# Transformers in a one-core kernel: weight and table loads get an issue-order edge behind a slot's moves, and the second transformer's feed-forward runs one slot earlier

## The chip, the cores and the metric

The kernel runs on one core of a Trainium2 chip. The metric is the device time of the whole program in microseconds (us), taken as the median of several runs. Before the change the median is 4267.34 us (three runs: 4264.73, 4267.34 and 4271.99). A profiled execution of the same program took 4258.36 us; its span, from the first instruction to the last, is 4256.7 us. All times inside the program below are counted from the start of that span.

The engines are named as the profile names them: PE multiplies matrices (PEld loads the weights for it), DVE, ACT and POOL work elementwise, and SP issues DMAs. DMAs can also be issued from the ACT and POOL queues.

## The reference

The input is a stream `x` of 4 rows of 512 tokens with 128 features, in float32. Four layers follow each other, each of the form `x = x + s * silu(f)`, where `s` comes from an attention-like block and `f` from a feed-forward-like block, both of the normalised `x`. The change touches two of these blocks, which are small transformers of their own. They differ in depth, number of heads and window:

| | "l2" (third layer) | "l3" (fourth layer) |
|---|---|---|
| depth | 6 | 2 |
| heads of 64 | 16 | 8 |
| attention window | 32 tokens | 64 tokens |

One layer of such a transformer, cut to what matters:

```
h = shift(x)                      # half of the features come from the token before
q, k, v = split(h @ Wqkv)
q = rotate(l2norm(q) * q_scale)   # cos/sin tables, xpos scaling
k = rotate(l2norm(k) * k_scale)
p = softmax(8 * q @ k.T)          # over the own window and the one before
x = x + (p @ v) @ Wo
h = layernorm(shift(x)) * g + b   # feed-forward
a, gate = split(h @ W1 + b1)
x = x + (a * gelu(gate)) @ W2 + b2
```

## The kernel before

The class `_Transformer` runs each of the two transformers in *slots*. A slot is one triple of layer `l`, row `b` (of 4) and group `gp` of 8 heads. "l2" has two groups (`GP` = 2) and so 6 x 4 x 2 = 48 slots; "l3" has one group (`GP` = 1) and 2 x 4 = 8 slots. Three Python generators make the work, and `transformer` (L707) merges them slot by slot:

- `queries_keys` (L1263) projects a slot's queries and keys (matmuls `S<-hb,l_wqk`), squares them on ACT (`sqp`), multiplies by two rotary tables on DVE (`l_rot<-S,l_tab` L1289, `rotp<-S,l_tab` L1291), adds on POOL (L1292), and normalises (`unit_length`, L1302, with DVE at L1316). Then eight DMAs, the *moves* (`l_qk<-l_rot`, L1323), put the heads where the attention needs them. There are eight for the queries and eight for the keys of a slot, so 896 in all; they are issued from SP.
- `attention` (L1463) works one slot behind. For each slot it first projects the values (`values`, L1326, matmuls `S<-l_wv,hb`), copies them out on ACT, and shifts them with DMAs `l_ve<-l_vo` (L1346 to L1350). Then come the scores (L1377), the softmax, the transposes (`S<-core,l_P`), the weighing with the values (`S<-l_ve,l_PT` and `S<-l_vo,l_PT`), the transposes back (`core,l_On`), and the output projection (`M<-l_OT,l_wo`). Each of these steps lags one or two units behind the scores, so a slot's attention ends early in the slot after.
- `feed_forward` (L1506) works on a row after its attention. Its matmuls are `S<-hb,l_k` and `S<-ffg,core` (layer norm), `S<-hb,l_w` (W1) and `M<-ffu,l_w` (W2).

In slot number i the loop of `transformer` gives `merge` the projection of slot i, the attention of slot i-1 and, from slot `GP + 2` on, the feed-forward. For "l3" the feed-forward of row r is therefore in slot r+3, and the loop has 11 slots. `merge` interleaves the generators by the weights they yield.

The written order is not the order on the engines. The framework that builds the program places each engine's instructions ahead of time, by its own model of when each is ready; the order in which they are written is a priority only. An instruction that waits for nothing, such as a load into a free buffer, so moves forward in its queue. What was placed once stands: on the chip each engine and each queue works strictly in that order, and waits on semaphores at its head.

Weights are loaded on first use by `part` (L1217): `l_wqk` (512 KB, two buffers), `l_wv` (256 KB, two buffers) and `l_wo` (256 KB, two buffers), all from SP. The feed-forward's `W1` and `W2` come from `ff_weights` (L1247), with one buffer each. The rotary tables (1024 KB each, one for queries and one for keys per layer, three buffers) are loaded by `tables` (L1235) from the ACT queue, and are multiplied by the layer's scale on DVE right after (L1243). PSUM has three two-bank tiles `S` and two one-bank tiles `M` for all of these matmuls.

Before "l2" starts, two 1 MB arrays (`away_x`, `away_s`) are written out from SP, and the transformer's column constants `l_cols` take memory that is free once `away_s` is written.

Of the kernel before, what the change touches and what calls it, by code (L numbers as in the profile page):

```python
# [38 lines left out]
class Net:  # L39
# [667 lines left out]
    def transformer(self, pre, depth, heads, window, consts):  # L707

        with ExitStack() as stack:
            pool = lambda name, bufs=1, **kw: stack.enter_context(self.pool(pre + name, bufs, **kw))
            pools = [pool("ps", 3, space=PSUM), pool("pm", 2, space=PSUM), pool("c"), pool("tab", 3), pool("w")]
            pools += [pool("qk", 4), pool("v", 2), pool("p", 2), pool("t", 2)]
            t = _Transformer(self, pre, heads, window, pools, consts)
            t.exp_tables()
            rows = [(l, b) for l in range(depth) for b in range(B)]
            passes = t.queries_keys(rows), t.attention(rows), t.feed_forward(rows)  # L720
            slots = len(rows) * t.GP
            for i in range(slots + t.GP + 2):
                run = []
                if i < slots:
                    run.append((until_none(passes[0]), 10.3))
                if 0 < i <= slots + 1:
                    run.append((until_none(passes[1]), t.attention_weight))
                if i >= t.GP + 2:
                    run.append((until_none(passes[2]), t.feed_forward_weights[i % t.GP]))
                merge(run)  # L730

# [435 lines left out]


class _Transformer:
    def __init__(self, net, pre, heads, window, pools, consts):  # L1170
        self.net, self.nc, self.a, self.pre = net, net.nc, net.a, pre
        self.heads, self.W, self.inner = heads, window, heads * 64
        self.GP = heads // 8
        self.NB = 128 // window
        self.split = self.NB == 4
        self.PS, self.PM, C, self.TB, self.WT, self.QK, self.VP, self.PP, self.TP = pools
        nc, a = self.nc, self.a
        self.T = 4 if self.split else 2
        self.NU = self.T * 64 // window
        self.cols = net.load(C, a[pre + "cols"], name=pre + "_cols")  # L1180
        k = net.load(C, a[consts][:, 0:256], name=pre + "_k", queue=nc.scalar)
        self.ones, self.cen = k[:, 0:128], k[:, 128:256]
        self.tiny = C.tile([128, 1], F32, name=pre + "_tiny")
        nc.vector.memset(self.tiny, 1e-36)
        n = NT // self.T
        self.mask = C.tile([128, n, 512], BF16, name=pre + "_mask")
        nc.gpsimd.dma_start(self.mask, a[consts][:, 256 : 256 + 512 * n].rearrange("p (t n) -> p t n", t=n))
        self.identb = C.tile([128, 128], BF16, name=pre + "_identb")
        nc.vector.tensor_copy(self.identb, net.ident)

        self.ve = [C.tile([128, self.NU, 1024 // self.NB], F32, name=f"{pre}_ve{i}") for i in range(2)]
        for i in range(2 if self.split else 1):
            for lo, hi in self.second():
                nc.gpsimd.memset(self.ve[i][lo:hi, 0, :], 0.0)
        self.made, self.weights = {}, {}

        self.attention_weight = 25.0
        self.feed_forward_weights = (1.7, 7.7) if self.GP == 2 else (9.4,)
        self.y = net.xn

    def second(self):
# [15 lines left out]
    def part(self, kind, l, gp):  # L1217
# [14 lines left out]
            self.weights[key] = t  # L1232
        return self.weights[key]

    def tables(self, l, i):  # L1235

        if ("tab", l, i) not in self.weights:
            nc, pre = self.nc, self.pre
            tab = self.TB.tile([128, 2, 2, S], F32, name=pre + "_tab")
            nc.scalar.dma_start(tab, self.a["k_rot_" + pre][:, 4 * i : 4 * i + 4, :].rearrange("p (m h) s -> p m h s", m=2))  # L1240
            for h in range(2):
                v = tab[:, :, h, :]
                nc.vector.tensor_scalar(v, v, self.col(l, 9 + 2 * i + h), None, ALU.mult)  # L1243
            self.weights["tab", l, i] = tab
        return self.weights["tab", l, i]

    def ff_weights(self, l):  # L1247
        if ("ff", l) not in self.weights:
# [14 lines left out]
    def queries_keys(self, rows):  # L1263


        net, nc, W = self.net, self.nc, self.W
        for l, b in rows:
            hb = net.shifted(net.tok(self.y, b), self.TP, 3)

            hk = hb.rearrange("p (u s k) -> p s u k", s=2, k=W)  # L1270
            for gp in range(self.GP):
                w = self.part("qk", l, gp)
                before = None
                made = []
                for i in range(2):
                    tab = self.tables(l, i)
                    t = self.TP.tile([128, 2, 2, S], F32, name=self.pre + "_rot", bufs=2)
                    sums = []
                    for g in range(2):
                        p = self.S2()  # L1280
                        for h in range(2):
                            c = 128 * (4 * g + 2 * i + h)
                            o = p[:, h, :]
                            net.mm(o.rearrange("p (s u k) -> p s u k", s=2, k=W) if i else o, w[:, c : c + 128], hk if i else hb)
                            yield 0.86
                        sq = self.TP.tile([128, 2, S], F32, name="sqp", bufs=3)
                        nc.scalar.activation(sq, p, AF.Square)  # L1287
                        nc.gpsimd.tensor_tensor(sq[:, 0, :], sq[:, 0, :], sq[:, 1, :], ALU.add)  # L1288
                        nc.vector.tensor_tensor(t[:, g], p, tab[:, 0], ALU.mult)  # L1289
                        m = self.TP.tile([128, 2, S], F32, name="rotp", bufs=1)  # L1290
                        nc.vector.tensor_tensor(m, p, tab[:, 1], ALU.mult)  # L1291
                        nc.gpsimd.tensor_tensor(t[:, g], t[:, g], m[:, ::-1, :], ALU.add)  # L1292
                        sums.append(sq)
                        if before:
                            made.append((yield from self.unit_length(*before)))
                            before = None
                    before = sums, t
                made.append((yield from self.unit_length(*before)))
                self.made[l, b, gp] = hb, made
                yield None  # L1300

    def unit_length(self, sums, t):  # L1302

        net, nc = self.net, self.nc
        p = self.S2()
        for g in range(2):
            net.mm(p[:, g, :], self.ones, sums[g][:, 0, :])
            yield 0.86  # L1310
        rn = self.TP.tile([128, 2, S], F32, name="rn", bufs=1)
        nc.scalar.activation(rn, p, AF.Ln, bias=self.tiny)  # L1312
        nc.scalar.activation(rn, rn, AF.Exp, scale=-0.5)  # L1313
        for g in range(2):

            nc.vector.scalar_tensor_tensor(  # L1316
                t[:, g], rn[:, g, :].unsqueeze(1).to_broadcast([128, 2, S]), 1e12, t[:, g], ALU.min, ALU.mult
            )
        out = self.QK.tile([128, 2, 2, S], F32, name=self.pre + "_qk")
        for r in range(4):  # L1320
            for h in range(2):
                x = 32 * (2 * (r % 2) + h)
                nc.sync.dma_start(out[x : x + 32, :, r // 2, :], t[32 * r : 32 * r + 32, :, h, :])  # L1323
        return out

    def values(self, w, hb, tp, ve):  # L1326
# [136 lines left out]
    def attention(self, rows):  # L1463
# [6 lines left out]
        for i in range(len(units) + 2):  # L1470
# [18 lines left out]
            if older:  # L1489
                if older["j"] == 0:  # L1490
                    OT = self.TP.tile([128, 4, 128 * T], F32, name=self.pre + "_OT", bufs=1)
                self.turn_back(older, OT)
                yield 0.9 if self.split else 0.45
                if older["j"] == 1:
                    wo = self.part("o", older["l"], older["gp"])
                    p = self.M()[:, 0 : 128 * T]
                    for t in range(4):
                        net.mm(p, wo[:, t, :], OT[:, t, :], t == 0, t == 3)
                        yield 0.86 if self.split else 0.43
                    ys = net.tok(self.y, older["b"])[:, 128 * T * older["tp"] : 128 * T * (older["tp"] + 1)]  # L1500
                    nc.vector.tensor_tensor(ys, ys, p, ALU.add)
                older.clear()
            if last:
                yield from self.weigh(last)

    def feed_forward(self, rows):  # L1506
        net, nc = self.net, self.nc
        for l, b in rows:
            w1, w2 = self.ff_weights(l)
            yb = net.tok(self.y, b)  # L1510
            hb = net.shifted(yb, self.TP, 3)
# [178 lines left out]
```

## Time and profile before

| | us |
|---|---|
| median of three runs | 4267.34 |
| profiled execution | 4258.36 |
| its span | 4256.7 |
| PE busy | 3632.9 (85%) |
| DVE busy | 2521.8 (59%) |
| ACT busy | 1832.3 (43%) |
| POOL busy | 1200.4 (28%) |
| "l2" runs from about | 1590 to 3690 |
| "l3" runs from about | 3774 to 4244 |

The key moves of a slot give a clock for the slots. The first one of "l2" starts at 1635.4 and the last at 3633.2: 47 slots in 1997.8 us, 42.5 us each. In "l3" the distances from one slot's key moves to the next are 45.5, 51.6, 53.0, 54.7, 54.9, 54.6 and 51.2 us, from 3811.6 to 4177.1; what is left after that takes until 4244.

In a row of the windows view the columns are the stretch, its length, the busy time of PE, PEld, DVE, ACT and POOL with the number of instructions, the granted share of the PE clock, the share of time the DMA engines were busy, and GB/s. In a timeline a row has its start, its length, the engine, the line, the operation, what it writes and reads, how often, and in brackets the idle time before it with what ended that.

### The profile page before, as it was taken

What the parts mean: (1) busy time and instruction counts of PE and PEld (TensorE: products, weight loads), DVE (VectorE), ACT (ScalarE), POOL (GpSimd) and SP (SyncE); (2) the same over time, 40 slices, a digit from 0 to 9 for tenths busy, and PEclk for the clock granted to TensorE, in tenths of its full rate; (3) what the DMA queues carried; (4) which work ended last, traced back from release to release, by engine and by line L of the source; (5) the groups of instructions that cost most, each with busy time, mean ns of one, the idle gap of its engine ahead of it and who ended that gap; (6) DMA issues with size and microseconds to landing.
All of it is one profiled execution on the core that took longest, in us unless ns stands there. A gap on an engine that the chain in (4) does not pass through costs nothing.

```text
span 4256.7 us, 105246 instructions
## 1 busy us (share of the span) xinstructions
PE 3632.9 (85%) x46765; PEld 1894.8 (45%) x46891; DVE 2521.8 (59%) x3429; ACT 1832.3 (43%) x2495; POOL 1200.4 (28%) x994
## 2 busy tenths in 40 slices
PE   7887999898999986888888888888888888768888
PEld 4554555344444433444444444444444444334444
DVE  6665555205433516677677777777667676447775
ACT  3344666331333343444444444444444444424554
POOL 1011444100111224333333433343333333033221
PEclk7678999996989988999999999999999999879999
DMA  1000000000000004334233424333333332222221
GB/s 35 7 24 26 1 1 1 28 10 7 1 3 2 1 15 113 85 81 106 70 89 98 95 67 120 70 86 94 86 73 92 87 85 69 75 85 68 58 63 43
DMA packets 123574, 236.11 MB, mean 55 GB/s; under 512 B 29625, under 2 KB 44129, under 8 KB 117729
## 3 DMA queue, kind: packets, MB, share of 16 engines
q1 hardware_dynamic: 114064, 209.58, 20.3%
q10 hardware_dynamic: 8624, 19.29, 1.4%
q8 instruction: 369, 6.05, 0.6%
q0 software_dynamic: 432, 0.51, 0.1%
q14 instruction: 85, 0.69, 0.1%
HBM read 50.08 MB, written 5.54 MB: 13 GB/s over the span
## 4 chain that ended last, share of the span: by engine, by line
PE 53%; DVE 16%; ACT 16%; issue 8%; POOL 3%; DMA 3%; SPq 1%; DVEq 0%; POOLq 0%; ACTq 0%
PE S L122 29%; PE M L122 8%; PE S L126 4%; PE S L1377 3%; PE o L1092 3%; DVE l_rot L1316 3%; DVE rotp L1291 3%; ACT l_P L581 3%; DVE l_rot L1289 2%; ACT l_PT L1412 2%; PE o L614 2%; ACT rn L1312 2%; POOL l_rot L1292 2%; ACT sqp L1287 1%; ACT l_P L1396 1%
## 5 line engine op out<-in xcount | busy, mean ns | idle before, releaser
L1292 POOL TENSOR_TENSOR l_rot<-l_rot,rotp 128x1024 f32<-128x1024 f32 x224 | 533.3, 2381 | 459.1 <-DVE rotp L1291 421.6
L1288 POOL TENSOR_TENSOR sqp<-sqp 128x512 f32<-128x512 f32 x224 | 315.6, 1410 | 1010.2 <-ACT sqp L1287 1009.6
L122 PE MATMUL S<-hb,l_wqk 128*128 128x512 f32 x896 | 501.4, 659 | 108.4 <-ACT l_vo L1344 32.3
L1287 ACT ACTIVATE sqp<-S 128x1024 f32<-128x1024 f32 x224 | 229.3, 1024 | 411.0 <-PE S L122 408.6
L1316 DVE SCALAR_TENSOR_TENSOR l_rot<-rn,l_rot 128x1024 f32<-128x1024 f32 x224 | 366.2, 1672 | 64.8 <-ACT rn L1313 62.3
L1289 DVE TENSOR_TENSOR l_rot<-S,l_tab 128x1024 f32<-128x1024 f32 x224 | 272.9, 1218 | 163.7 <-ACT sqp L1287 161.8
L126 PE MATMUL S<-core,l_P 128*128 128x128 f32 x1856 | 269.5, 288 | 57.3 <-DVE rotp L1291 13.5
L122 PE MATMUL S<-l_KT,l_QT 32*128 32x256 f32 (+7 forms) x1536 | 261.9, 505 | 34.8 <-ACT l_P L1114 14.2
L126 PEld LDWEIGHTS S<-core,l_P 128*128 128x128 f32 x1856 | 211.3, 146 | 177.2 <-issue 67.4
L1291 DVE TENSOR_TENSOR rotp<-S,l_tab 128x1024 f32<-128x1024 f32 x224 | 271.6, 1213 | 22.0 <-POOL l_rot L1292 21.8
L122 PE MATMUL S<-sqp,l_k 128*128 128x512 f32 x448 | 241.7, 633 | 33.3 <-POOL sqp L1288 24.9
L1114 ACT ACTIVATE l_P<-S 128x1024 f32<-128x1024 f32 x160 | 156.7, 1022 | 254.6 <-PE S L122 254.5
L1377 PE MATMUL S<-l_qk 64*32 64x64 f32 (+1 forms) x13312 | 222.1, 236 | 43.3 <-issue 34.3
L122 PEld LDWEIGHTS S<-hb,l_wqk 128*128 128x128 f32 x896 | 150.1, 199 | 244.0 <-issue 102.2
L122 PE MATMUL S<-l_wv,hb 128*64 128x256 f32 (+1 forms) x1600 | 237.1, 403 | 7.8 <-ACT rn L1312 2.4
L1377 PEld LDWEIGHTS S<-l_qk 64*32 64x32 f32 (+1 forms) x13312 | 174.1, 110 | 154.5 <-issue 151.0
L1412 ACT COPY l_PT<-S 128x1024 f32<-128x1024 f32 x128 | 129.5, 1012 | 250.1 <-PE S L126 250.0
L1067 DVE TENSOR_REDUCE l_mx<-S 128x2 f32<-128x768 f32 (+1 forms) x192 | 154.9, 863 | 134.1 <-PE S L1006 134.1
L1398 DVE TENSOR_REDUCE rs<-l_P 128x16 f32<-128x1024 f32 (+1 forms) x128 | 155.8, 1217 | 124.2 <-ACT l_P L1396 124.1
L122 PE MATMUL M<-l_OT,l_wo 128*128 128x512 f32 (+1 forms) x512 | 222.7, 546 | 4.1 <-ACT l_OT L1461 2.2
L1118 POOL TENSOR_SCALAR_AFFINE_SELECT l_P<-l_P 128x256 f32<-128x256 f32 x256 | 99.4, 406 | 409.9 <-ACT l_P L1114 405.1
L1387 DVE TENSOR_REDUCE mx<-S 128x16 f32<-128x1024 f32 (+1 forms) x128 | 155.7, 1217 | 98.7 <-PE S L1377 98.5
(359 smaller groups left out, 6619.9 us busy)
## 6 DMA issues: line engine op xcount, KB each, us to landing
l_qk<-l_rot SPq DMA_DIRECT2D x896, 128.0 KB
l_ve<-l_vo SPq DMA_DIRECT2D x112, 256.0 KB
l_ve<-l_vo SPq DMA_DIRECT2D x96, 224.0 KB
l_tab<-in_k_rot_l ACTq DMA_DIRECT2D x16, 1024.0 KB
l_wqk<-in_l2Wqkv SPq DMA_DIRECT2D x12, 512.0 KB
l_wv<-in_l2Wqkv SPq DMA_DIRECT2D x12, 256.0 KB
l_wo<-in_l2Wo SPq DMA_DIRECT2D x12, 256.0 KB
l_ve<-l_vo SPq DMA_DIRECT2D x24, 128.0 KB
```

The lines of the kernel that those rows point to most:

```text
L122: self.nc.tensor.matmul(out, lhsT, rhs, start=start, stop=stop)
L126: self.nc.tensor.transpose(out, in_, self.ident[:n, :n])
L1114: nc.scalar.activation(P[u], s[u], AF.Exp, scale=scale)
L1287: nc.scalar.activation(sq, p, AF.Square)
L1288: nc.gpsimd.tensor_tensor(sq[:, 0, :], sq[:, 0, :], sq[:, 1, :], ALU.add)
L1289: nc.vector.tensor_tensor(t[:, g], p, tab[:, 0], ALU.mult)
L1291: nc.vector.tensor_tensor(m, p, tab[:, 1], ALU.mult)
L1292: nc.gpsimd.tensor_tensor(t[:, g], t[:, g], m[:, ::-1, :], ALU.add)
L1316: nc.vector.scalar_tensor_tensor(t[:, g], rn[:, g, :].unsqueeze(1).to_broadcast([128, 2, S]), 1e12, t[:, g], ALU.min, ALU.mult)
L1377: net.nc.tensor.matmul(sv[W * bl : W * bl + W, e, t, g, :].rearrange("p (s k) -> p s k", s=2), qk[0][r, g, j, W * c : W * c + W], kw, star ...
L1398: nc.vector.tensor_reduce(rs, P.rearrange("p t g e k -> p (t g e) k"), axis=AX.X, op=ALU.add)
L1412: self.nc.scalar.copy(u["PT"], t)
```

## The change

Five edits:

1. Tables are loaded by a new function `load_tables`, from SP instead of ACT. The scaling on DVE stays in `tables`, at first use.
2. A new function `ahead` is called at the end of each slot's projection, inside `issue_after`: every DMA that it traces on SP is placed behind the slot's last move. No completion is waited for; it is an edge of issue order alone. After the slot of row 3 it loads the next layer's `l_wqk` of this group and the table of this group's number (for "l3", both tables). After the slots of row 0 it loads this layer's `l_wv` of this group. `l_wo` follows after (row 0, group 1) and (row 1, group 0), for "l3" after row 0.
3. `ahead` also asks for the feed-forward's weights after row 2. `feed_forward` has asked for the same weights in an earlier place of the merged order (slot 8l+4 against 8l+5 in "l2"; in "l3" at 60% of the same slot), so this adds nothing.
4. In "l3" the feed-forward begins in slot 2 instead of slot 3, with a first `yield 14.0` out of a weight of 23.4 (before: 9.4), so that a row's feed-forward follows in the last 40% of the slot in which its attention ends. The loop has 10 slots instead of 11. In "l2" the slots stay as they were.
5. An `assert` states that the row's attention has been written before; it makes no instruction.

The first layer's `l_wqk` and tables are still loaded without the edge, on first use.

```diff
-            for i in range(slots + t.GP + 2):
+            for i in range(slots + 4 if t.GP == 2 else slots + 2):
...
-                if i >= t.GP + 2:
+                if i >= (4 if t.GP == 2 else 2):
...
-        self.feed_forward_weights = (1.7, 7.7) if self.GP == 2 else (9.4,)
+        self.feed_forward_weights = (1.7, 7.7) if self.GP == 2 else (23.4,)
...
+    def load_tables(self, l, i):
+        if ("tab", l, i) not in self.weights:
+            tab = self.TB.tile([128, 2, 2, S], F32, name=self.pre + "_tab")
+            self.nc.sync.dma_start(
+                tab, self.a["k_rot_" + self.pre][:, 4 * i : 4 * i + 4, :].rearrange("p (m h) s -> p m h s", m=2)
+            )
+            self.weights["tab", l, i] = tab, []
+        return self.weights["tab", l, i]
+
     def tables(self, l, i):
 
-        if ("tab", l, i) not in self.weights:
-            nc, pre = self.nc, self.pre
-            tab = self.TB.tile([128, 2, 2, S], F32, name=pre + "_tab")
-            nc.scalar.dma_start(tab, self.a["k_rot_" + pre][:, 4 * i : 4 * i + 4, :].rearrange("p (m h) s -> p m h s", m=2))
+        tab, ready = self.load_tables(l, i)
+        if not ready:
             for h in range(2):
                 v = tab[:, :, h, :]
-                nc.vector.tensor_scalar(v, v, self.col(l, 9 + 2 * i + h), None, ALU.mult)
-            self.weights["tab", l, i] = tab
-        return self.weights["tab", l, i]
+                self.nc.vector.tensor_scalar(v, v, self.col(l, 9 + 2 * i + h), None, ALU.mult)
+            ready.append(True)
+        return tab
+
+    def ahead(self, l, b, gp):
+
+        last = gp == self.GP - 1
+        if b == B - 1 and l + 1 < self.depth:
+            self.part("qk", l + 1, gp)
+            for i in (gp,) if self.GP == 2 else (0, 1):
+                self.load_tables(l + 1, i)
+        if b == 0:
+            self.part("v", l, gp)
+        if self.GP == 1 and b == 0:
+            self.part("o", l, 0)
+        if self.GP == 2 and (b, gp) in ((0, 1), (1, 0)):
+            self.part("o", l, b)
+        if b == 2 and last:
+            self.ff_weights(l)
...
                 self.made[l, b, gp] = hb, made
+                with net.tc.issue_after(self.move.ins):
+                    self.ahead(l, b, gp)
                 yield None
...
-                nc.sync.dma_start(out[x : x + 32, :, r // 2, :], t[32 * r : 32 * r + 32, :, h, :])
+                self.move = nc.sync.dma_start(out[x : x + 32, :, r // 2, :], t[32 * r : 32 * r + 32, :, h, :])
...
         for l, b in rows:
+            if self.GP == 1:
+
+                yield 14.0
+            assert (l, b) in self.attended
             w1, w2 = self.ff_weights(l)
```

More of the change, by code (lines that the diff above doesn't have):

```diff
@@ L716, in transformer @@
             pools += [pool("qk", 4), pool("v", 2), pool("p", 2), pool("t", 2)]
-            t = _Transformer(self, pre, heads, window, pools, consts)
+            t = _Transformer(self, pre, depth, heads, window, pools, consts)
             t.exp_tables()
@@ L1169, with __init__ @@
 class _Transformer:
-    def __init__(self, net, pre, heads, window, pools, consts):
+    def __init__(self, net, pre, depth, heads, window, pools, consts):
         self.net, self.nc, self.a, self.pre = net, net.nc, net.a, pre
-        self.heads, self.W, self.inner = heads, window, heads * 64
+        self.depth, self.heads, self.W, self.inner = depth, heads, window, heads * 64
         self.GP = heads // 8
@@ L1194, in __init__ @@
                 nc.gpsimd.memset(self.ve[i][lo:hi, 0, :], 0.0)
-        self.made, self.weights = {}, {}
+        self.made, self.weights, self.attended = {}, {}, set()
         self.attention_weight = 25.0
-        self.feed_forward_weights = (1.7, 7.7) if self.GP == 2 else (9.4,)
+        self.feed_forward_weights = (1.7, 7.7) if self.GP == 2 else (23.4,)
         self.y = net.xn
@@ L1501, in attention @@
                     nc.vector.tensor_tensor(ys, ys, p, ALU.add)
+                    if (older["gp"], older["tp"]) == (self.GP - 1, n - 1):
+                        self.attended.add((older["l"], older["b"]))
                 older.clear()
```

## The prediction

> **What bounds the kernel now.** I read the page first (busy shares and the chain that ended last), then the windows by stage, then the waits, then timelines of the queues and engines that the change touches.
>
> ```profile
> PE 3632.9 (85%) x46765; PEld 1894.8 (45%) x46891; DVE 2521.8 (59%) x3429; ACT 1832.3 (43%) x2495; POOL 1200.4 (28%) x994
> ...
> PE 53%; DVE 16%; ACT 16%; issue 8%; POOL 3%; DMA 3%; SPq 1%; DVEq 0%; POOLq 0%; ACTq 0%
> ```
>
> PE is the busiest engine and holds half of the chain; DMA and SP's queue hold 4% together. That is the first warning: a change that orders loads has little waiting to remove.
>
> ```profile
> 1635.00:3633.00 1998.00, 1711.03 (x29006) 875.71 (x29095) 1406.26 (x1505) 902.92 (x1019) 721.05 (x420) 0.98 0.36 86
> ...
> 3812.00:3857.00 45.00, 35.12 (x314) 20.30 (x316) 32.42 (x39) 20.17 (x25) 15.44 (x9) 0.92 0.29 68
> 3857.00:3909.00 52.00, 40.49 (x352) 24.42 (x356) 35.66 (x42) 21.95 (x29) 15.80 (x9) 0.87 0.25 59
> 3909.00:4177.00 268.00, 234.09 (x1880) 133.60 (x1901) 199.38 (x240) 144.03 (x175) 73.85 (x49) 0.96 0.27 63
> 4177.00:4219.00 42.00, 39.33 (x409) 25.49 (x410) 25.09 (x37) 22.66 (x34) 0.09 (x1) 1.00 0.21 48
> 4219.00:4244.00 25.00, 20.91 (x41) 8.15 (x40) 8.44 (x15) 10.50 (x13) 0.00 (x0) 0.86 0.00 0
> ```
>
> The first number after the length is PE's busy time: 86% through "l2", 87% in the full slots of "l3", 78% in its filling (3812 to 3909), 94% and 84% in its draining. So both transformers are near PE's pace, with about 6 us idle in a slot of 42.
>
> ```profile
> SPq L1323 <- DVE l_rot L1316: 817.4, 86, 26.2
> ...
> SPq L1224 <- PE S L122: 87.8, 5, 19.4
> ```
>
> SP waits for `l_wqk`'s buffer at the head of its queue (87.8 us, 5 times), but the moves behind are not held: by the timeline each batch leaves within 0.4 us of the DVE result (L1316) it carries, and summed over all 112 batches the lateness is 3 us. What the edge would protect is not being lost.
>
> **A. The values' weights come late.** This is the large term. `l_wv` was loaded a layer ahead; now it may leave only behind the key moves of the slot whose values come next.
>
> ```profile
> 1958.76 0.38 SPq L1231 DMA_DIRECT2D l_wo<-in_l2Wo  x1
> 1959.94 12.58 SPq L1323 DMA_DIRECT2D l_qk<-l_rot  x16
> 1975.69 1.20 SPq L1346 DMA_DIRECT2D l_ve<-l_vo  x2
> ```
>
> ```profile
> 1964.12 0.65 PE L122 MATMUL S<-l_wv,hb 128*64 128x256 f32 x4
> 1964.71 1.98 PE L122 MATMUL S<-hb,l_w 128*128 128x512 f32 x4
> 1966.62 1.51 PE L122 MATMUL S<-l_wv,hb 128*64 128x256 f32 x12
> ...
> 1972.56 1.95 PE L122 MATMUL S<-l_wv,hb 128*64 128x256 f32 x16
> ```
>
> The last move leaves SP at 1972.5, `l_wv` at 1973.0 (0.53 us is the median of its issue rows). A 1024 KB table took 4.9 us from its issue (1892.76) to the DVE row that it released (1897.65); 256 KB lie between a quarter of that and all of it, and I take 3 us, so 1976. The values' matmuls ran from 1964.12 to 1974.50: they would start 12 us late, 4.1 us of PE work (0.65 + 1.51 + 1.95). The planner sees this and puts other ready work there: W1 (5.6 us), the next slot's queries (2 us a tile), transposes (1.1 each way), weighing (2.5). These cover nearly all 12 us, but PSUM has only three `S` tiles, and PE's order is then fixed, so a landing later than planned stops everything behind it: scores, transposes, the ACT copy `l_vo`, the `l_ve` moves. Bounds a slot: at worst all 4.1 us; at best a gain, because the next slot's queries now wait for that copy (PE waits for `l_vo` 36.7 us in 47 waits over "l2", up to two of 0.9 in a slot), say -2 us. I take 1.25, nearer to cover than to loss, since the named work is ready. Twelve slots: +15 (-24 to +49). "l3" has two; the first falls where PE already stands 4.4 us: +2 (0 to +8).
>
> **B. Start of "l2".** Both tables (2 MB) now stand on SP's queue, probably ahead of `away_s` (1 MB), whose landing frees `l_cols`; DVE stood 10.7 us for `away_s` and began the scaling at 1605.66. At 1 MB per 4.9 us, queueing behind up to 2 MB would cost 9.8, less what the two queues already shared. I take +5 (-4, if `away_s` goes first, to +7).
> [...]
>
> **C. Layer boundaries of "l2" (five).**
>
> ```profile
> 1897.65 1.42 DVE L1243 TENSOR_SCALAR l_tab<-l_tab,l_cols 128x1024 f32<-128x1024 f32 x2 [1.12 <-DMA l_tab<-in_k_rot_l]
> ```
>
> DVE waits for tables 8.4 us in "l2" (9 waits); ACT stands 1.3 us before each of five table issues (its work ends 1891.5, the issue is 1892.76): 6 us; SP's `W2` waits cost the moves 0.4 us each and stay. If all of it goes: -14. I take -9, as DVE may still meet a table early. Against it: `l_wqk` and a table (1.5 MB, some 7 us) now follow directly on the key moves in two slots a layer, ahead of the `l_ve` moves and of the dense scores and weighing. There PE stands with "issue" as releaser (91 us over "l2"); in the slots where a table was in flight this idle time is 1.3 to 4.9 us, 2.6 on average, and about 1.2 in their like without one. One more such slot a layer: 5 x 1.4 = +7. Together -2 (-14, all waits gone at no cost, to +7, none gone).
> [...]
>
> **D. Start of "l3".** PE waits 13.4 us for the first `l_wqk`, which shares the engines with everything that floated forward. With less ahead: -2 (-4 to +2).
>
> **E. Layer boundary of "l3".** `l_wqk` and both tables (2.5 MB) are now issued after slot 3's moves (SP free at 3966.9), where slot 4's queries had begun at 3958.8. They start 12 us late; attention and feed-forward cover it: +4 (0 to +12, all of it).
>
> **F. Feed-forward a slot earlier in "l3".**
>
> ```profile
> 4217.57 1.56 PE L122 MATMUL M<-l_OT,l_wo 128*128 128x256 f32 x6 [0.16 <-ACT l_OT L1461]
> 4220.10 5.42 PE L122 MATMUL S<-hb,l_w 128*128 128x512 f32 x12 [0.97 <-DVE hb L1522]
> ...
> 4232.62 8.38 PE L122 MATMUL S<-hb,l_w 128*128 128x512 f32 x12 [2.80 <-DVE hb L1522]
> 4240.84 2.85 PE L122 MATMUL M<-ffu,l_w 128*128 128x512 f32 x6
> ```
>
> After the attention's end (4219.1) two feed-forwards follow, one of about 10 us of PE work too many. Slot 2 takes the first row's instead (51.6 us to some 54.7, and slot 3 from 53.0): +5. The drain loses 10 us of work, but the last layer norm then has no cover (2.8 us of gap already): -8. In the second layer the queries no longer follow directly on a feed-forward: PE waits 1.2 us for `hb` and 1.6 for `xn` in four slots, 11 us at most, of which I take half: -5. Together -8 (-20 to +6).
>
> **Sum.** 15 + 2 + 5 - 2 - 2 + 4 - 8 = +14 us on the profiled execution of 4258.4 us, 4272. The median of the runs shown is 9 us above that execution, so I forecast 4281, +0.3%. Less than 8.5 us (0.2%) can't be told from no change.
>
> **The rivals.**
>
> 1. *Faster: the late values are a better order.* The same deferral frees PSUM for the next slot's queries and removes waits for `l_vo`. For it: 36.7 us of such waits. Against it: the chain through 1964 to 1974 is PE itself. At -2 us a slot, A is -24, the sum -25, the time 4242. It decides once a slot gains more than 0.6 us (A below -7.5).
> 2. *PE stalls at the values.* The planner thinks `l_wv` lands sooner than it does; DVE's waits for tables show that it was hopeful before (up to 1.8 us each). At 4.1 us a slot, A is +49, the sum +48 and the time 4315.
> 3. *Absorbed.* Idle time elsewhere takes the delay, A and B come to nothing: 14 - 20 = -6, 4261, within the bound. The edge then does nothing, as the moves were never late.
>
> **How the numbers follow.** Forecast (A between 0.8 and 2.5 us a slot) 0.32, its own range 4276 to 4296; rival 2 0.15; rival 1 0.33, a share of it for F at its best end; rival 3 0.20. So slower 0.47, same 0.20, faster 0.33. The range reaches down below rival 1's point and up beyond rival 2's: 4232 to 4322, one in ten left out on each side.
>
> **What would show it.** SP's timeline: `l_wv` right behind 16 moves, tables on SP. The rows `S<-l_wv,hb` 10 us or more behind the key moves' start instead of 3 before it; a wait of PE for `DMA l_wv` of several us in total speaks for rival 2, none with shorter slots 0 and 1 of each layer for rival 1. The first DVE scaling of "l2" after 1610 shows B. One feed-forward after the last `l_wo` row, and "l3" ending 8 us sooner after its start, shows F. I am wrong if the planner rearranges whole slots away from the loads, which no row of before can show.

## The result, and the profile after

The changed kernel takes 4438.53 us (median of 4 runs, 4423.68 to 4452.01) against 4266.03 us before: the ratio is 1.0404, 95% interval 1.0367 to 1.0441. The execution profiled took 4439.52 us, with a span of 4437.8 us. Slower was the side I had given most weight to, but 4281 us was forecast and 4322 us was the range's end: the loss is 172 us, not 14.

First, where in the program it lies. From the two timelines I took the first query matmul of "l2", the first and last key moves of each transformer (the second eight of the 16 moves `l_qk<-l_rot` of a slot), and the last matmul, all in us:

| stretch | before | after | difference |
|---|---|---|---|
| "l2": first query matmul to first key move | 37.8 | 33.7 | -4.1 |
| "l2": first to last key move | 1997.9 | 2146.5 | +148.6 |
| from there to the first key move of "l3" | 178.4 | 175.7 | -2.7 |
| "l3": first to last key move | 365.5 | 408.3 | +42.8 |
| "l3": from there to the last matmul | 66.6 | 62.4 | -4.2 |
| sum | 2646.1 | 2826.8 | +180.7 |

These stretches leave out what comes ahead of "l2", which the change doesn't touch. The page's first line and one of its groups, of the kernel after:

```profile
PE 3660.8 (82%) x46765; PEld 1915.7 (43%) x46891; DVE 2515.8 (57%) x3429; ACT 1817.1 (41%) x2485; POOL 1191.4 (27%) x994
...
L122 PE MATMUL S<-l_wv,hb 128*64 128x256 f32 (+1 forms) x1600 | 249.9, 422 | 184.8 <-DMA l_wv<-in_l2Wqkv 152.6
```

The matmuls are the same in number, but PE's share of the span fell from 85% to 82%: it waits. The group of the values' matmuls says for what: 184.8 us of idle time ahead of them, 152.6 of it for `l_wv`. Of the waits of PE from "l2" on (total, times, longest) these four grew most:

```profile
PE S L122 <- DMA l_wv<-in_l2Wqkv: 152.6, 12, 15.1
...
PE S L122 <- DMA l_wv<-in_l3Wqkv: 29.5, 2, 17.7
PE S L126 <- ACT l_P L1421: 26.2, 6, 6.3
...
PE S L122 <- DMA l_wqk<-in_l3Wqkv: 23.7, 2, 13.4
```

The window that answers to "l2" in the prediction has PE busy for 81% of the time (1744.04 of 2146.00) instead of 86%:

```profile
1632.00:3778.00 2146.00, 1744.04 (x29025) 892.55 (x29120) 1402.11 (x1506) 901.75 (x1019) 715.89 (x420) 0.94 0.33 81
```

The lines of the waits stand for twelve waits of 12.7 us on average in "l2", two of `l_wv` in "l3", a second one for `l_wqk` (at the layer boundary of "l3"; the one at its start was there before), and transposes (L126) that wait for the exponentials (12.1 us in 8 times before). All other waits of PE together are some 50 us shorter than before. One of the twelve, first SP's queue, then PE's timeline, in the slot that the prediction looked at:

```profile
1963.85 15.55 SPq L1348 DMA_DIRECT2D l_qk<-l_rot  x16
1979.45 0.58 SPq L1228 DMA_DIRECT2D l_wv<-in_l2Wqkv  x1
```

```profile
1968.50 1.98 PE L122 MATMUL S<-hb,l_wqk 128*128 128x512 f32 x4
1982.52 1.12 PE L122 MATMUL S<-l_wv,hb 128*64 128x256 f32 x4 [12.03 <-DMA l_wv<-in_l2Wqkv]
1983.57 4.81 PE L122 MATMUL S<-hb,l_w 128*128 128x512 f32 x8
1988.31 1.51 PE L122 MATMUL S<-l_wv,hb 128*64 128x256 f32 x10
```

The load leaves right behind the 16th move and lands some 3 us later, as forecast. What was not forecast is what PE does meanwhile: it is through with the queries at 1970.5 and stands for 12.03 us at the first values' matmul, with eight W1 matmuls (`hb,l_w`) that need no `l_wv` next in its queue. The wait is made of 3.8 us until DVE has the rotated keys (1974.3), 5.1 us for the eight key moves, 0.6 us for the issue of `l_wv` and 2.5 us until it is there.

### The profile page after: what moved, and what is told of

It reads as the page before. It is cut to its first block, busy times and chain, and to the rows that moved or that the text cites. A ratio compares the mean times of both kernels' runs of the same rounds, so it can differ in the third digit from the quotient of the medians.

```text
span 4437.8 us, 105206 instructions
## 1 busy us (share of the span) xinstructions
PE 3660.8 (82%) x46765; PEld 1915.7 (43%) x46891; DVE 2515.8 (57%) x3429; ACT 1817.1 (41%) x2485; POOL 1191.4 (27%) x994
## 5 line engine op out<-in xcount | busy, mean ns | idle before, releaser
L122 PE MATMUL S<-hb,l_wqk 128*128 128x512 f32 x896 | 496.9, 653 | 96.5 <-ACT l_vo L1369 25.4
L122 PE MATMUL S<-l_wv,hb 128*64 128x256 f32 (+1 forms) x1600 | 249.9, 422 | 184.8 <-DMA l_wv<-in_l2Wqkv 152.6
L1310 ACT ACTIVATE sqp<-S 128x1024 f32<-128x1024 f32 x224 | 229.1, 1023 | 419.5 <-PE S L122 417.6
L126 PE MATMUL S<-core,l_P 128*128 128x128 f32 x1856 | 273.0, 290 | 78.8 <-ACT l_P L1421 26.2
L126 PEld LDWEIGHTS S<-core,l_P 128*128 128x128 f32 x1856 | 214.3, 147 | 207.6 <-issue 66.6
L122 PE MATMUL S<-l_KT,l_QT 32*128 32x256 f32 (+7 forms) x1536 | 268.0, 516 | 34.4 <-ACT l_P L1114 14.2
L122 PEld LDWEIGHTS S<-l_wv,hb 128*64 128x64 f32 (+1 forms) x1600 | 120.8, 148 | 348.1 <-issue 271.7
L122 PE MATMUL S<-sqp,l_k 128*128 128x512 f32 x448 | 242.0, 629 | 22.8 <-POOL sqp L1311 18.0
L122 PEld LDWEIGHTS S<-hb,l_wqk 128*128 128x128 f32 x896 | 150.2, 198 | 221.9 <-issue 90.9
L122 PE MATMUL M<-l_OT,l_wo 128*128 128x512 f32 (+1 forms) x512 | 221.8, 547 | 5.6 <-ACT l_OT L1486 4.0
```

Source lines behind the costliest of these rows:

```text
L122: self.nc.tensor.matmul(out, lhsT, rhs, start=start, stop=stop)
L126: self.nc.tensor.transpose(out, in_, self.ident[:n, :n])
```

## The experiments

The runs are numbered in the order in which they were made, and are told by subject. Each median is compared with runs of the kernel before that were made beside it (medians 4264 to 4266 us).

### What the late `l_wv` costs

**Run 1.** Undone alone, in the changed kernel:

```diff
     def ahead(self, l, b, gp):
...
-        if b == 0:
-            self.part("v", l, gp)
...
                 w = self.part("qk", l, gp)
+                if b == 0:
+                    self.part("v", l, gp)
```

> The changed kernel, with one part undone: l_wv is asked for at the start of its slot's queries and floats, so it leaves SP a slot ahead of the key moves again; all other edges, the tables on SP and the early feed-forward stay. Theory 1 (the late l_wv alone: TensorE stands 152.6 us for it in l2 and 29.5 us in l3): 4439 - 182 = 4257 us, between 4245 and 4290, and the waits of PE for DMA l_wv are gone. Theory 2 (the other edges and the tables on SP's queue carry a large part, 50 us or more): above 4310 us. Theory 3 (the new order of instructions is what costs, and the waits would only show elsewhere): above 4400 us.

Measured: 4298.26 us, ratio to before 1.0077 (1.0061 to 1.0094). No wait for `l_wv` is left among PE's larger ones. 140 of the 172 us are this one load, and theory 3 falls: nothing else in the order took the waits over. But 4298 is above the forecast range of theory 1 (4290): other parts of the change cost some 34 us.

**Run 2.** Done alone, in the kernel before:

```diff
                 self.made[l, b, gp] = hb, made
+                with net.tc.issue_after(self.move.ins):
+                    if b == 0:
+                        self.part("v", l, gp)
```

> The kernel before, with one part of the change alone: l_wv leaves behind the key moves of the first row's slots; no other edge, tables on ACT, feed-forward where it was. Theory 1: 4266 + 153 + 18 to 30 = 4437 to 4449 us, between 4410 and 4460. Theory 2 (the parts add up, and this is a minor one): below 4370 us. If the other parts hide some of the wait, this run is slower than the changed kernel.

Measured: 4419.44 us, 1.0358 (1.0341 to 1.0375); PE waits 155.0 us in 12 waits in "l2" and 19.9 in two in "l3". This edge alone makes 155 us. Here theory 1 holds; in run 1 its range was missed by 8 us, which are those other parts.

**Run 4** moves the same edge, in the changed kernel, from the last key move to the last query move:

```diff
                         if before:
                             made.append((yield from self.unit_length(*before)))
+                            if b == 0:
+                                with net.tc.issue_after(self.move.ins):
+                                    self.part("v", l, gp)
                             before = None
```

> The changed kernel with the edge of l_wv at the last of the 8 query moves instead of the last of the 8 key moves, so that it leaves some 10 us sooner and is still behind moves. By the profile of after TensorE stands from 1970.5 to 1982.5 in such a slot; l_wv would leave at about 1969.5 and land at 1972.5. Theory 1 (time follows the landing, one for one, because the order on TensorE stays as it is): 2 to 3 us of wait a slot are left of 12.7, so 14 slots times 10 us come back: about 4300 us, between 4280 and 4330. Rival (an edge of any kind breaks the overlap, or the planner moves the values up as far again): 4400 us or more. Rival (anything behind moves but in time is as good as none): 4250 to 4275 us.

Measured: 4315.02 us, 1.0113 (1.0096 to 1.0131): 123 us come back. SP's queue, and below it PE's timeline and one line of its waits, in this kernel:

```profile
1951.90 6.05 SPq L1349 DMA_DIRECT2D l_qk<-l_rot  x8
1957.99 0.58 SPq L1228 DMA_DIRECT2D l_wv<-in_l2Wqkv  x1
1962.39 5.08 SPq L1349 DMA_DIRECT2D l_qk<-l_rot  x8
```

```profile
1956.56 1.98 PE L122 MATMUL S<-hb,l_wqk 128*128 128x512 f32 x4
...
1961.16 0.65 PE L122 MATMUL S<-l_wv,hb 128*64 128x256 f32 x4 [2.62 <-DMA l_wv<-in_l2Wqkv]
1961.74 5.46 PE L122 MATMUL S<-hb,l_w 128*128 128x512 f32 x8
1967.13 1.51 PE L122 MATMUL S<-l_wv,hb 128*64 128x256 f32 x10
```

```profile
PE S L122 <- DMA l_wv<-in_l2Wqkv: 28.9, 12, 5.9
```

PE's order in this slot is that of the changed kernel, instruction for instruction; only the landing is earlier, and the waits go from 152.6 to 28.9 us. So the time follows the landing, and the order does not answer it: it is the same for a load that leaves before or behind the eight key moves.

**Run 8.** Was there work to put into the wait? This run is the changed kernel, keeps the load late and writes the values later. The yield is a weight for the interleaving, not a wait on the chip:

```diff
                 if j == 0:
+                    if self.split and u["b"] == 0:
+                        yield 8.0
                     u["ve"] = self.ve[gp if self.split else tp]
```

> The changed kernel, with l_wv as late as there, but the values of the first row's slots put later in the program, so that on TensorE the feed-forward's W1 and W2 or its layer norm and one to three more tiles of the queries stand ahead of them (before them in the changed kernel: none of these). It tests whether there was work to cover the wait, as I had assumed. Theory 1 (cover exists, the order did not use it): 4 to 9 us of 12.7 a slot come back in the 12 slots of l2: 4330 to 4390 us. Rival (the wait is handed on to the scores, which now end the slot): 4420 us or more.

Measured: 4279.99 us, 1.0040 (1.0015 to 1.0065), more than theory 1 had hoped for: 158 of the 172 us. PE's timeline of this kernel in the same slot; its `l_wv` leaves SP at 1972.4:

```profile
1963.43 1.88 PE L122 MATMUL S<-hb,l_w 128*128 128x512 f32 x4
1966.29 1.95 PE L122 MATMUL S<-hb,l_w 128*128 128x512 f32 x4 [0.98 <-DVE l_On L1466]
...
1970.65 1.02 PE L122 MATMUL M<-ffu,l_w 128*128 128x512 f32 x2
1971.64 1.98 PE L122 MATMUL S<-hb,l_wqk 128*128 128x512 f32 x4
1973.46 1.88 PE L122 MATMUL M<-ffu,l_w 128*128 128x512 f32 x4
1975.47 0.65 PE L122 MATMUL S<-l_wv,hb 128*64 128x256 f32 x4
```

W1, W2 and the queries now fill the time, and the values start without a wait. The cover that the prediction named did exist; only the order that was placed did not use it. Not all of the 158 us are cover, though: run 10 below has the same edit without a late load, and gains 21 us by it.

### The feed-forward of "l3"

**Run 3.** Done alone, in the kernel before:

```diff
-            for i in range(slots + t.GP + 2):
+            for i in range(slots + 4 if t.GP == 2 else slots + 2):
...
-        self.feed_forward_weights = (1.7, 7.7) if self.GP == 2 else (9.4,)
+        self.feed_forward_weights = (1.7, 7.7) if self.GP == 2 else (23.4,)
...
         for l, b in rows:
+            if self.GP == 1:
+                yield 14.0
             w1, w2 = self.ff_weights(l)
```

> The kernel before, with only the feed-forward of l3 a slot earlier. In the changed kernel l3 is 37 us longer, of which waits for l_wv are 29.5 and the wait for l_wqk at the layer boundary 13.4: together 43, so the moved feed-forward gains some 5 us if these are all. Theory 1: 4255 to 4264 us (my prediction's term said -8: 4258). Rival: the new waits of TensorE for l_P in three slots of l3 (16 us) belong to the moved feed-forward, and it costs: 4270 to 4285 us.

Measured: 4283.47 us, 1.0043 (1.0025 to 1.0061): it costs 19 us, and the rival is right. PE, then ACT, in a full slot of "l3" of this kernel:

```profile
4158.59 1.10 PE L1377 MATMUL S<-l_qk 64*64 64x128 f32 x32
4166.02 1.76 PE L126 MATMUL S<-core,l_P 128*128 128x128 f32 x7 [6.33 <-ACT l_P L1396]
```

```profile
4164.91 1.06 ACT L1396 ACTIVATE l_P<-l_P 128x1024 f32<-128x1024 f32 x1 [7.60 <-DVE l_P L1391]
```

The first scores of the slot (L1377) go through DVE's maximum and subtraction and ACT's exponential before they can be transposed (L126), and PE stands 6.33 us. In the kernel before, W1 of the previous row stood at this place, and the transposes began without a wait:

```profile
4085.79 1.10 PE L1377 MATMUL S<-l_qk 64*64 64x128 f32 x30
4086.82 1.98 PE L122 MATMUL S<-hb,l_w 128*128 128x512 f32 x4
...
4090.81 1.88 PE L122 MATMUL S<-hb,l_w 128*85 128x512 f32 x4
...
4094.09 1.09 PE L126 MATMUL S<-core,l_P 128*128 128x128 f32 x8
```

The wait of 6.33 us stands in five slots of run 3; all waits of PE for `l_P` from 3700 us on are 43.0 us there, and 12.1 us in the kernel before. In its new slot W1 can't stand between scores and transposes: the feed-forward follows its own attention, whose last residual is written only later in the slot. From first to last key move "l3" grows from 365.5 to 390.8 us, in each of slots 2 to 7, and the end after the last key move shrinks by 1.3 us alone.

**Run 6.** The other way round, in the changed kernel:

```diff
-            for i in range(slots + 4 if t.GP == 2 else slots + 2):
+            for i in range(slots + t.GP + 2):
...
-        self.feed_forward_weights = (1.7, 7.7) if self.GP == 2 else (23.4,)
+        self.feed_forward_weights = (1.7, 7.7) if self.GP == 2 else (9.4,)
...
-            if self.GP == 1:
-
-                yield 14.0
```

> The changed kernel with one part undone: the feed-forward of l3 in its old slot; l_wv stays late. Theory 1 (the parts add up; alone the moved feed-forward cost 19 us): 4438 - 19 = 4419 us, between 4405 and 4428. Rival (its cost is covered by the slots that wait for l_wv anyway): 4432 to 4442 us. My prediction's term (the move gains 8 us) would make it 4446 us.

Measured: 4419.83 us, 1.0367 (1.0330 to 1.0404). The 19 us come off as a whole; the two losses add up.

**Run 12.** Is it the place or the pause? Run 3's kernel with the shortest pause at which the feed-forward still follows its attention:

```diff
-        self.feed_forward_weights = (1.7, 7.7) if self.GP == 2 else (23.4,)
+        self.feed_forward_weights = (1.7, 7.7) if self.GP == 2 else (15.4,)
...
-                yield 14.0
+                yield 6.0
```

> The kernel before with the feed-forward of l3 a slot earlier, as in the third run, but its pause 6 instead of 14, the least at which it still follows its attention in the program. In the third run TensorE stands 6.3 us in each of five slots between a slot's first scores and their transposes, where W1 stood before. In this order W1 still does not reach that place. Theory (it is the first scores that lost their cover, which no feed-forward of the same slot's attention can give): still 6 us in each slot, 4278 to 4292 us. Rival (the pause of 14 crowds the feed-forward into the slot's end): 4258 to 4268 us.

Measured: 4322.88 us, 1.0135 (1.0113 to 1.0157), worse by another 39 us, which neither had expected. In this kernel's timeline of PE the wait at the first transposes is still there, and longer:

```profile
4060.53 1.30 PE L1377 MATMUL S<-l_qk 64*64 64x128 f32 x34
4070.07 1.75 PE L126 MATMUL S<-core,l_P 128*128 128x128 f32 x7 [8.24 <-ACT l_P L1396]
```

So it is not the pause of 14 that causes this wait; it stays with the place. Why the shorter pause costs still more was not followed up.

### The other loads

**Run 5.** What is left of the change when `l_wv` (as in run 1), the feed-forward (as in run 6) and all edges in "l3" are taken back:

```diff
-                with net.tc.issue_after(self.move.ins):
-                    self.ahead(l, b, gp)
+                if self.GP == 2:
+                    with net.tc.issue_after(self.move.ins):
+                        self.ahead(l, b, gp)
```

> The changed kernel without its two parts that were shown to cost: l_wv leaves early as in the first run, and the feed-forward of l3 has its old slot; l3 has no edges. What stays is in l2: l_wqk, tables, l_wo, W1 and W2 behind a slot's moves, tables on SP's queue. Theory 1 (these are worth little either way; my terms B and C sum to +3): 4264 + 3, between 4255 and 4275 us. Rival (the last slot of a layer, 3 to 5 us shorter in the profile after, is a real gain of the edge): 4240 to 4254 us. Rival (loads that queue together behind the moves cost 15 us or more): 4279 us or more.

Measured: 4267.98 us, 1.0002 (0.9982 to 1.0023). The edges of "l2" and the tables on SP are worth nothing that can be told. From key move to key move the slot that ends a layer is 4.2 us shorter with them (44.5 against 48.7 us, mean of the five layers that have a next one), and the two behind it are 2.9 and 1.9 us longer.

**Runs 7 and 14** try the boundary of "l3", on run 1's kernel. First `l_wqk` alone, three slots earlier:

```diff
-        if b == B - 1 and l + 1 < self.depth:
+        if b == (B - 1 if self.GP == 2 else 0) and l + 1 < self.depth:
             self.part("qk", l + 1, gp)
+        if b == B - 1 and l + 1 < self.depth:
             for i in (gp,) if self.GP == 2 else (0, 1):
```

> The first run's kernel (l_wv early, all else as changed), with the second l3 layer's l_wqk behind the moves of the first layer's first row instead of its last; the tables stay behind the last row's. In the first run TensorE waits 11 us for this l_wqk at the boundary. Theory 1: 4298 - 11 = 4287 us, between 4280 and 4292. Rival (the tables behind it end the same wait): 4294 us or more.

Measured: 4295.91 us, 1.0073 (1.0044 to 1.0101), the same as run 1: the rival. Run 1's waits of VectorE at this boundary show what stands behind `l_wqk`:

```profile
DVE l_tab L1250 <- DMA l_tab<-in_k_rot_l: 12.8, 2, 11.7
```

Then (run 14) `l_wqk` and both tables without an edge:

```diff
-        if b == B - 1 and l + 1 < self.depth:
+        if self.GP == 2 and b == B - 1 and l + 1 < self.depth:
```

> The first run's kernel (l_wv early, all else as changed), with l_wqk and the tables of the second l3 layer without an edge, so that they leave when their buffers come free. Theory (term E: they were late by a wait of 11 to 13 us that TensorE and VectorE shared; the slot there is 7 us longer than in the third run's): 4298 - 7 to 14 = 4284 to 4291 us. Rival (those 14 us are elsewhere, in l2's edges or in the first slots of l3): 4294 us or more.

Measured: 4291.83 us, 1.0074 (1.0050 to 1.0098). By the times this is not to be told from run 1. In the profile the waits of PE for `l_wqk` of "l3" are down from 24.8 to 10.7 us and the stretch between the key moves of "l3" from 399.4 to 390.7 us, which is run 3's 390.8. So the 8.7 us at the boundary rest on two profiles and not on a timed difference.

### Later values without the change

**Runs 9 and 10.** Run 8's kernel was faster in "l2" than the kernel before (1979.2 us between the key moves, against 1997.9). Is that the order alone? First the later values on top of run 5's kernel, then in the kernel before; the edit is run 8's:

> The kernel of the fifth run (edges in l2 alone, l_wv early, feed-forward of l3 in its old slot), and the values of the first row's slots put later as in the eighth. In the eighth run l3 began 19 us sooner than in the kernel before though 23 us of waits for l_wv were left in l2, while its l3 lost 20 us for the feed-forward and 29 us for l_wv. Theory (the later values are worth something by themselves, even with l_wv there in time): 4266 - 19 = 4247 us, less if the 23 us come back too: 4225 to 4255. Rival (later values only cover a wait, and without one they gain nothing): 4260 us or more.

> The kernel before with nothing but the later values in the first row's slots of l2: no edge, tables on ACT. Tells whether the edges have a part in what the run of the same call with both gains. If the gain is the order's alone: the same as that run within 8 us, 4225 to 4255. If the edges are what makes it a gain: 4260 us or more.

Measured: 4264.04 us, 0.9995 (0.9981 to 1.0010), and 4245.11 us, 0.9952 (0.9929 to 0.9975). The order alone gains 0.5%; in run 9 that gain is lost. The edges on the other loads do not explain this by themselves: run 8 has them too, and differs from run 9 in "l2" only in that `l_wv` leaves late, yet between the key moves it takes 1979.2 us and run 9 2014.5. Of these 35 us, 23 lie between the second and the third key moves of a layer; what costs them was not found.

**Run 11.** The kernel before with later values in all slots of "l2", not the first row's only:

```diff
                 if j == 0:
+                    if self.split:
+                        yield 8.0
                     u["ve"] = self.ve[gp if self.split else tp]
```

> The kernel before with the later values in all slots of l2, not only in the first row's. The slots with a feed-forward's second half, 45 to 47 us long, have W1 and W2 to put ahead of the values as the first row's have. Theory (the gain is in how values and feed-forward alternate, 2 to 3 us a slot): 4266 - 4 times the gain of the first row's: 4180 to 4240. Rival (the first row's slots are special, or the scores at the end of a slot become late): 4266 or more.

Measured: 4143.08 us, 0.9716 (0.9694 to 0.9737). That is 123 us less than the kernel before, from this edit alone and none of the change, and beyond the best that I had expected. Of PE's waits in this kernel three lines:

```profile
PE S L122 <- DVE hb L90: 77.6, 28, 4.3
PE S L122 <- ACT l_PT L1412: 33.3, 66, 1.1
PE S L122 <- DVE rotp L1291: 23.8, 9, 7.0
```

A layer takes 317 to 322 us from last key move to last key move, against 336 to 349. The slots with W1 go from 45 to 52 us down to 41 to 44, those without it stay at 36 to 41. Waits for `rotp` at L122 are half of what they were, and "issue" at L122 is no longer among the first twenty lines. In the kernel before these were the two longest:

```profile
PE S L122 <- issue: 61.6, 38, 4.5
PE S L122 <- DVE rotp L1291: 47.2, 44, 7.1
```

Now `hb` is the largest wait. The trace shows where the idle time at "issue" stands: between the first and the last key move of "l2" in the kernel before, 41 such gaps are over 0.7 us, and counted in all records of PE, PEld and their queue (58648 there, 229 times 256) they are 255, 1023, 1278 or 2555 apart and the like, always within 5 of a multiple of 256. From "l2" on the kernel before has 61.6 us at "issue" in 38 waits at L122 and 34.3 us in 41 at L1377; run 11 has 1.4 us in 2 and 11.8 us in 17. Why most multiples of 256 have no such gap, and why there is less of this idle time in run 11's order, was not tested.

**Run 13.** The same line in the whole changed kernel, with the late `l_wv`, all edges and the moved feed-forward:

> The changed kernel whole (l_wv late, all edges, the moved feed-forward), with the values put later in all slots of l2, as in the run at 4143 us without any of the change. Theory (in l2 a late l_wv costs next to nothing once other work stands ahead of it; l3 still loses 19 us for the feed-forward, about 14 at the layer boundary and up to 29 for l_wv): 4143 + 33 to 62, so 4176 to 4210 us. Rival (the landing is still the bound in the first row's slots, 12 of them at 5 us or more): 4260 us or more.

Measured: 4179.29 us, 0.9806 (0.9784 to 0.9829). Of its waits of PE:

```profile
PE S L122 <- DMA l_wv<-in_l3Wqkv: 29.6, 2, 17.7
PE S L126 <- ACT l_P L1421: 26.2, 6, 6.3
PE S L122 <- DMA l_wv<-in_l2Wqkv: 24.5, 4, 12.0
```

With this order the late load costs 24.5 us of waits in "l2" instead of 152.6, half of them in the very first slot. The same change that loses 172 us on one order of instructions loses 36 on another (4179.29 against 4143.08, each in its own group of runs).

## Why the prediction was wrong

The sum of terms was +14. What the runs give for each, in the stretches of the table above:

| term | forecast (bounds) | measured | from |
|---|---|---|---|
| A, `l_wv` in "l2" | +15 (-24 to +49) | +134.8 | changed kernel less run 1, between key moves of "l2" |
| A, `l_wv` in "l3" | +2 (0 to +8) | +8.9 | the same, between key moves of "l3" |
| B, start of "l2" | +5 (-4 to +7) | -4.1 | table |
| C, boundaries of "l2" | -2 (-14 to +7) | +13.8 (+7.8 in run 5) | run 1 less before, between key moves of "l2" |
| D, start of "l3" | -2 (-4 to +2) | -2.7 | table |
| E, boundary of "l3" | +4 (0 to +12) | +8.7 | run 1 less run 14, between key moves of "l3" |
| F, feed-forward | -8 (-20 to +6) | +25.3 - 4.2 = +21.1 | run 3 less before, and the table's last stretch |

They sum to 180.5, the table's 180.7. Each is a difference of two profiles: runs 1, 5, 7 and 14, which have the same text for "l2", take 2011.7, 2005.7, 2012.3 and 2004.7 us between its key moves, so A in "l2" and C are known to some 8 us. F is a mixed sum, as its last stretch is the changed kernel's; run 3 alone costs 19 us by its times.

**A failed, and its step is "at worst all 4.1 us".** The bound was the PE work of the values that would come late. But PE, which works in a fixed order and stood at its head, lost the time until the landing, whatever it was going to do there: landing less arrival, 1982.5 - 1970.5 = 12.0 us. The 12 us of lateness stood in the prediction's own text, as what "the planner" would cover; the cover was assumed in the step "The planner sees this and puts other ready work there". The work was there, as run 8 shows, but in the changed kernel's order only two more query matmuls had come ahead of the values in this slot (four in a row at 1968.50, two before). Rival 2 had the right mechanism, "PE stalls at the values", with the price of 4.1 us: at the 12.7 us measured its A would have been 152 and its time about 4418.

**F failed in its sign.** The step "The drain loses 10 us of work" counted what the end saves, and "the queries no longer follow directly on a feed-forward" what the slots save. Left out was what W1 had covered where it stood: the way of a slot's first scores through DVE and ACT, 6.33 us in five slots of run 3. The "+5" for the filling was 13.1 (slots 2 and 3 go from 51.6 and 53.0 to 60.1 and 57.6 in run 3), the "-5" for the second layer was +12.3 (slots 4 to 7 together), and the end gave 1.3 there instead of 8.

**B** went to its lower end: SP issued `away_s` (1595.24) ahead of both tables (1595.64 and 1601.42), and the first scaling stood at the same time as before although "l2" began 3 us later (its first load leaves at 1594.15, before at 1590.8). DVE in the kernel before, then after:

```profile
1605.66 4.98 DVE L1243 TENSOR_SCALAR l_tab<-l_tab,l_cols 128x1024 f32<-128x1024 f32 x3 [2.76 <-DMA l_wv<-in_l2Wqkv]
```

```profile
1605.78 2.64 DVE L1250 TENSOR_SCALAR l_tab<-l_tab,l_cols 128x1024 f32<-128x1024 f32 x2 [4.28 <-DMA l_cols<-in_l2cols]
```

The wait ahead of it is for `l_cols`, not for a table, so the forecast delay did not come. Of the 4.1 us gained, 2.0 are here: the first rotation follows two scalings (at 1608.52) and not three (at 1610.56), which the forecast had not in view. The rest was not taken apart.

**C, D and E.** In C the waits of DVE for tables in "l2" are gone, as forecast, and "issue" at L122, which was to rise, fell (61.6 to 31.1 us); still C came out at or above its upper bound. The 7 to 14 us more between the key moves of "l2" are the balance of longer first slots and a shorter last slot of a layer (run 5), and no run took them apart. With the shorter start and the shorter way to "l3" they make nothing (run 5). D and E lie within their bounds; E's wait is the one foreseen.

"What the edge would protect is not being lost" held: no run with edges gained from them.

## What to carry to other kernels

An order edge on a load moves the landing, and here PE, with its fixed order, lost the whole distance from arrival to landing (12.0 us in the slot shown), not the work that waits (4.1 us): read where the consumer stands in its engine's order, and subtract. Before work is moved to another slot, ask what it covers where it stands; here the feed-forward between scores and their transposes covered 6.3 us of softmax a slot, and without it "l3" grew by 25.3 us from first to last key move. And before a load is pulled or pinned, try the order of its consumer: putting the values later brought the waits for a late load from 152.6 to 24.5 us in "l2", and without the change made the kernel 2.8% faster than before.

## What was not expected of the hardware

After the 12.03 us wait shown above the clock is low. Windows of the changed kernel around it (the first number after the length is PE's busy time; the third from the end is the granted clock):

```profile
1960.00:1970.50 10.50, 10.48 (x149) 4.71 (x147) 9.04 (x8) 5.01 (x6) 5.25 (x3) 1.00 0.44 100
1970.50:1982.50 12.00, 0.00 (x0) 0.01 (x1) 6.07 (x6) 2.31 (x2) 3.60 (x2) 0.71 0.46 111
1982.50:1986.00 3.50, 3.48 (x7) 1.48 (x8) 0.00 (x0) 0.00 (x0) 0.00 (x0) 0.52 0.00 0
1986.00:1990.00 4.00, 4.00 (x17) 1.75 (x16) 1.50 (x2) 1.38 (x2) 0.00 (x0) 1.00 0.00 0
```

For the 3.5 us after the wait TensorE has a granted clock of 0.52, and is back at 1.00 in the next window: about 1.7 us of work lost (3.5 times 0.48); the first four matmuls of the values take 1.12 us there, and 0.65 at 1964.12 in the kernel before. In the 3.5 us after each of the other eleven waits in "l2" it is 0.50, and 0.63 to 0.86 in the 3.5 us behind those. Twelve times the 1.7 us of the first is an estimate of 20 us. PE's busy time agrees in size: between the key moves of "l2" it is 1744.4 us, and 1724.3 in run 1, whose load alone is early. It is no proof, since it differs with the order too (1746.8 in run 9, which has no wait for `l_wv`). In time the late load did not cost more than its waits (134.8 us against 152.6), as PE's other waits are some 35 us shorter in the changed kernel than in run 1. Behind a shorter wait the clock was low too: in run 4, after the 2.62 us shown there, the granted clock is 0.72 from 1961 to 1964 us and 0.78 from 1964 to 1968. The prediction's sum had no such term.

Also, the first query matmul of "l2" stands between 1582.5 and 1607.0 us in the profiles of these kernels, though no edit touches the work ahead of it. That is 24 us of spread from that part alone, and the reason why the stretches above are counted from there.
